# A fused attention layer in Strassen quads: normalised inputs laid out token by token, and four output products carried over in PSUM

## The chip, the core and the metric

The kernel runs on one core of a Trainium2 chip. A core has five engines with queues of their own: TensorE (matrix products, written PE in the profile, its weight loads PEld), VectorE (DVE), ScalarE (ACT), GpSimd (POOL) and SyncE (SP). They share SBUF, the working memory of 128 partitions, and PSUM, eight banks that TensorE writes its products to. DMA engines move data between SBUF and DRAM. The metric is device time in microseconds (us), lower is better.

## The reference

Eight sequences of 256 tokens with 512 features, all in float32. Cut to what matters:

```python
x = hidden_states                                  # (8, 256, 512)
xn = (x - mean(x)) / sqrt(var(x) + 1e-5)           # over the 512 features
q, k, v = xn @ wq.T, xn @ wk.T, xn @ wv.T          # 32, 8 and 8 heads of 128
q, k = rope(q), rope(k)
scores = q @ k.T / sqrt(128) * scale + causal      # one k head for 4 q heads
s = softmax(scores) @ v                            # (8, 256, 4096)
s = s @ wo.T                                       # back to 512 features
# experts: 4 of rank 16, each token takes the best two
gates = softmax(top2(xn @ router_w.T))
delta = sum_e gates_e * 4.0 * (xn @ A_e.T) @ B_e.T
out = x + s * silu(delta)
```

## The kernel before

The sequences are handled in four blocks of two (`tb`, 0 to 3). Within a block the heads go in eight groups (`g`, 0 to 7; one key head and four query heads).

**Products in quads.** Projections and the output projection use a scheme of seven products instead of eight for a 2 x 2 split (Strassen in Winograd's form). A quad of 512 output features for two sequences is cut into 2 x 2 by features of the input (`half`) and by sequence (`b`); the sums of weights (S1 to S4) are formed once, kept in DRAM and loaded again by the later blocks. The input's sums are formed by `add_up` into `XT`. In `quad` (lines 575 to 656) products 1, 2 and 3 read the normalised input `XB` itself and products 4 to 7 a sum in `XT`. Names in the trace: `pa`, `pe` and `pd` are the three PSUM banks of a quad, followed by q, k or v. One product is four matmuls of 128 x 128 x 256 that the profile shows as eight records, since a float32 matmul runs in two passes. For queries and keys the input is the moving operand, which streams through the array; for values (`rows`) it is the stationary one, loaded as weights.

**How the normalised input comes.** `norm` (lines 318 to 478) loads `x`, takes mean and variance and normalises, tokens on partitions. The products need the features on partitions. In the first block TensorE transposes and ScalarE copies from PSUM (`turn`, `read`). In the later three VectorE transposes 32 x 32 blocks (`turn_blocks`), `spread` writes them to DRAM (`turned`, four DMAs a sequence) and `gather` loads them to `XB` (four DMAs a sequence). These DMAs are issued by SyncE, in one queue with the stores and loads that turn the softmax's result (`there<-blocks`, `pT<-there`). `XB` has one buffer: `gather` for the next block waits until the last product of this block that reads `XB` is done.

**Attention.** `softmax` computes scores (`sc`), exponentials and sums, transposes 32 x 32 blocks and sends them through DRAM to `pT`; `values` multiplies with `v` (`av`, copied to `a`).

**Output projection.** `out_project` (lines 944 to 1020) forms for each group seven products `po` in PSUM, each of which is added to an accumulator `acc` 1 to 7 in SBUF (`add_up`: ScalarE copies in the first group, VectorE adds after that). At the end of a block `put_together` combines the seven accumulators into the four quarters of the output, multiplies with the gates `g` (loaded from DRAM) and adds the input `xf`. For the last group of the last block `last_products` (lines 1022 to 1161) does this by hand: the accumulators of the first seven groups are put together (`put`) while TensorE still works, and the last group's products stay in PSUM: 1, 6, 7 and 4 follow each other in one bank `oa`, copied aside by ScalarE in between; 2 stands in `oe`, 5 in `od`, and 3 comes in two halves (`o3_0`, `o3_1`). `result` adds a sum of these to the accumulator, multiplies by the gate and adds the input, three VectorE operations.

**What sets the order.** `Plan` (lines 170 to 257) is a planner that runs when the program is built. TensorE's pieces are laid in an order written out by hand (lines 1413 to 1459); every other job gets a due time from the pieces that need it, an estimated duration and a lag, and is put into its engine's queue when a small simulation finds it ready. The estimates fix only the order. `hold` and `Room` keep account of buffers, `ps_mm` with four banks among them (tag `mm`). Engines work through their queues strictly in this order.

`experts` computes the router and the experts; `route` reads `XB` as the stationary operand (`lme`).

Nearly all instructions are recorded by one helper, so the profile gives line 118 for them; tiles and operations tell them apart.

Of the kernel before, what the change touches and what calls it, by code (L numbers as in the profile page):

```python
# [260 lines left out]
def layer(ctx: ExitStack, tc: tile.TileContext, x, wquad, woquad, raT, bT, table, out):  # L261
# [53 lines left out]

    def norm(tb):

# [47 lines left out]
        def new_acts():  # L367
            acts[tb] = (
                one.tile([P, NB, 2, 2, S], F32, tag="XB", name=f"XB{tb}"),
                one.tile([P, 4, 2, S], F32, tag="XT", name=f"XT{tb}"),  # L370
            )

        def read(b, half):
            if b == half == 0:
                new_acts()
            nc.scalar.copy(acts[tb][0][:, b, half], box["p", b, half])

        def turn_blocks(t):
# [3 lines left out]
                to.rearrange("p (q k t s) -> p t k q s", q=NQ, k=DC, t=2)[:, t % 2],  # L382
# [14 lines left out]
        def gather(b):  # L397
            if b == 0:
                new_acts()
            to = acts[tb][0][:, b].rearrange("p h c (t a s) -> p a (h c t) s", t=2, a=NQ)  # L400
            for a in range(NQ):
                nc.sync.dma_start(
                    out=to[:, a],
                    in_=box["there", b][:, :, a, :].rearrange("q r (k s) -> (q r) k s", s=BLK),
                )

        def add_up(i):
            XB, XT = acts[tb]
            b11, b12, b21, b22 = (XB[:, b, h] for h in range(2) for b in range(NB))
# [35 lines left out]
        if tb:  # L445
            for b in range(NB):
# [6 lines left out]
                    add("sp", 2.4, lambda b=b: gather(b), after=[out_] + reads[:1],  # L453
# [121 lines left out]
    def quad(tb, which, out, room, rows, name):  # L575
# [15 lines left out]
        def product(bank, i, half, b, t, first):  # L591
# [3 lines left out]
            xb = acts[tb][0][:, b, half] if t is None else acts[tb][1][:, t]  # L595
# [172 lines left out]
    free_p = [None]  # L768
# [175 lines left out]
    def out_project(tb, g):  # L944
# [19 lines left out]
        for i, (to, a, b, op) in enumerate(Features.steps):  # L964
# [4 lines left out]
            )  # L969
        if (tb, g) == (NTB - 1, KV - 1):  # L970
# [3 lines left out]
        def product(k, a, w):  # L974
            box = {}

            def work():
                ps = box["ps"] = ps_mm.tile([P, 2, 2 * P], F32, tag="mm", name=f"po{n}_{k}")
                for t in range(2):
                    for h in range(2):  # L980
                        nc.tensor.matmul(
                            ps[:, t, :], lhsT=abox[a]["a"][:, h, bass.ts(t, P)],
                            rhs=wbox[w][:, h, :], start=t == h == 0, stop=h == 1,
# [12 lines left out]

            h = hold("mm")
            p = add("pe", 1.73, work, after=[a_done[a], w_done[w]], opens=[h], closes=[ah[a], wh[w]])
            if g == 0:
# [20 lines left out]
        return [pieces[k] for k in (1, 2, 6, 5, 7, 4, 3)]  # L1020

    def last_products(n, abox, ah, a_done, wbox, wh, w_done):

# [4 lines left out]
        turn = []  # L1028

        def put(to, a, b):  # L1030
            turn[:] = [
                dve(lambda: nc.vector.tensor_add(M[to]["s"], M[a]["s"], M[b]["s"]),
                    turn + [M[k]["done"] for k in (to, a, b)])
            ]
            M[to]["done"] = turn[0]
# [455 lines left out]
```

## Time and profile before

| | |
|---|---|
| time, median of three runs | 1338.13 us (1336.35 to 1342.35) |
| profiled execution | 1336.8 us, its span 1334.9 us |
| instructions | 20259 |
| matmuls of queries, keys and values that read `XB` | 1152 records of 128 x 256 |
| matmuls that read `XT` | 1536 records |
| DMA traffic | 282.14 MB, 211 GB/s |
| DMA packets | 143402, of them under 512 bytes 41856 |
| loads `XB<-turned` | 24 of 128 KB, median 4.9 us from issue to landing |
| loads `pT<-there` | 128 of 384 KB, median 5.5 us |

The span is the time from the first to the last instruction that the profile shows; the rest of the execution's time lies around it. "Records" are the entries of the profile: a float32 matmul has two. A busy time counts overlapping records of an engine once. A record's duration is its latency; the next one starts before it ends, so the pace of a stream is read from how long a run of records takes together. The granted clock of TensorE was 0.999 of full speed over the execution.

### The profile page before, as it was taken

The page shows a single profiled execution, that of the slowest core. Times are in us where ns is not written, and L with a number is a line of the kernel's source. Part 1 is how long each engine was busy: PE and PEld are TensorE (multiplying, and loading weights), DVE is VectorE, ACT ScalarE, POOL GpSimd, SP SyncE. Part 2 cuts the span into 40 slices and gives each one's busy share as a digit, 9 for nine tenths or more (in the row PEclk, how much of TensorE's full clock was granted, in tenths as well). Part 3 has the DMA queues.
Part 4 walks back from the last instruction along what each step waited for, and adds up shares of the span by engine and source line. Part 5 has one row for each costly group of instructions (what it writes and reads, how often), then busy time and mean ns, then how long its engine had stood idle before and what let it go on. Part 6 is the DMA issues. An engine that isn't in the chain of part 4 may idle for free.

```text
span 1334.9 us, 20259 instructions
## 1 busy us (share of the span) xinstructions
PE 1323.2 (99%) x6488; PEld 1166.7 (87%) x6488; DVE 1046.9 (78%) x2515; ACT 700.5 (52%) x1896; POOL 314.6 (24%) x579
## 2 busy tenths in 40 slices
PE   8999999999999999999999999999999999999998
PEld 7888888888889888888888988888888888888886
DVE  6798888986978658688597875968858787685987
ACT  3485455554645546465454564546544455544751
POOL 2332222222221122221222212222122221222010
PEclk9999999999999999999999999999999999999999
DMA  6497666696766765768766666576866676566583
GB/s 213 159 294 245 208 219 217 203 266 217 229 191 207 214 212 177 228 205 246 220 192 221 209 209 206 174 249 201 235 222 192 211 221 208 180 194 198 161 293 109
DMA packets 143402, 282.14 MB, mean 211 GB/s; under 512 B 41856, under 2 KB 81920, under 8 KB 143296
## 3 DMA queue, kind: packets, MB, share of 16 engines
q0 software_dynamic: 45760, 149.98, 36.5%
q1 hardware_dynamic: 97312, 130.20, 31.4%
q8 instruction: 53, 0.87, 0.3%
q10 hardware_dynamic: 224, 0.66, 0.2%
q14 instruction: 53, 0.43, 0.1%
HBM read 197.94 MB, written 82.84 MB: 210 GB/s over the span
## 4 chain that ended last, share of the span: by engine, by line
PE 97%; DVE 1%; DMA 1%; SPq 1%; issue 0%; DVEq 0%; ACT 0%
PE po L118 28%; PE paq L118 17%; PE av L118 12%; PE sc L118 10%; PE pdq L118 8%; PE peq L118 4%; PE pav L118 4%; PE pak L118 4%; PE pdk L118 2%; PE pdv L118 2%; PE dle L118 1%; PE pev L118 1%; PE lme L118 1%; PE pek L118 1%; SPq L118 1%; DMA pT<-there 1%
## 5 line engine op out<-in xcount | busy, mean ns | idle before, releaser
L118 ACT ACTIVATE p<-z,least 128x256 f32<-128x256 f32 (+7 forms) x512 | 207.2, 406 | 138.0 <-DVE least L118 107.1
L118 PE MATMUL po<-wo,a 128*128 128x256 f32 x992 | 233.5, 379 | 0.0
L118 PEld LDWEIGHTS po<-wo,a 128*128 128x128 f32 x992 | 186.6, 190 | 22.9
L118 PE MATMUL av<-pT,v 128*128 128x256 f32 x768 | 186.4, 380 | 1.5 <-DMA pT<-there 1.4
L118 DVE CUSTOM_DVE_ANT_0 z<-sc,tab 128x256 f32<-128x256 f32 (+7 forms) x512 | 132.9, 301 | 67.1 <-PE sc L118 63.9
L118 PE MATMUL paq<-XT,w 128*128 128x256 f32 x768 | 181.7, 379 | 0.0
L118 PE MATMUL po<-wo,s 128*128 128x256 f32 x744 | 177.5, 382 | 0.0
L118 PEld LDWEIGHTS sc<-kk,qTq 128*128 128x128 f32 x1024 | 159.0, 191 | 12.8 <-DVE p L118 0.8
L118 DVE TENSOR_TENSOR acc<-acc,po 128x512 f32<-128x512 f32 x189 | 127.8, 677 | 52.7 <-PE po L118 51.8
L118 PE MATMUL sc<-kk,qTq 128*128 128x256 f32 (+7 forms) x1024 | 167.7, 302 | 0.0
L118 PEld LDWEIGHTS av<-pT,v 128*128 128x128 f32 x768 | 145.3, 190 | 22.1 <-issue 2.7
L118 PEld LDWEIGHTS paq<-XT,w 128*128 128x128 f32 x768 | 145.0, 190 | 18.9 <-ACT p1q L118 0.2
L118 ACT COPY a<-av 128x512 f32<-128x512 f32 x128 | 74.6, 583 | 163.3 <-PE av L118 162.8
L118 PEld LDWEIGHTS po<-wo,s 128*128 128x128 f32 x744 | 139.4, 190 | 22.6 <-issue 5.3
L118 POOL DMA_DIRECT2D w<-sums x144 | 79.0, 549 | 334.9 <-PE paq L118 129.7
L118 POOL DMA_DIRECT2D w<-in_wquad_dram x148 | 81.0, 548 | 259.7 <-PE paq L118 84.8
L118 ACT COPY swq<-cq 64x1024 f32<-64x1024 f32 x128 | 133.6, 1044 | 4.6 <-DVE kk L118 2.3
L118 DVE STREAM_TRANSPOSE blocks<-p 128x1024 f32<-128x1024 f32 (+1 forms) x128 | 122.8, 965 | 3.9 <-DMA there<-blocks 2.0
L118 ACT ACTIVATE p<-p,total 128x160 f32<-128x160 f32 (+4 forms) x320 | 91.9, 363 | 27.2 <-DVE total L118 26.5
L118 DVE TENSOR_TENSOR qTq<-cq,tab 128x1024 f32<-128x1024 f32 x64 | 77.7, 1213 | 29.8 <-ACT cq L118 29.6
L118 ACT ACTIVATION_READ_ACCUMULATOR p<-z,least 128x1 f32 x512 | 95.9, 187 | 0.0
L118 POOL DMA_DIRECT2D wo<-in_woquad_dram x104 | 57.2, 551 | 130.3 <-PE po L118 125.1
(138 smaller groups left out, 1905.7 us busy)
## 6 DMA issues: line engine op xcount, KB each, us to landing
there<-blocks SPq DMA_DIRECT2D x256, 192.0 KB, 4.2
pT<-there SPq DMA_DIRECT2D x128, 384.0 KB, 5.5
w<-in_wquad_dram POOLq DMA_DIRECT2D x148, 256.0 KB, 4.5
w<-sums POOLq DMA_DIRECT2D x144, 256.0 KB, 4.2
wo<-in_woquad_dram POOLq DMA_DIRECT2D x104, 256.0 KB, 5.0
wo<-osums POOLq DMA_DIRECT2D x96, 256.0 KB, 4.6
sums<-w POOLq DMA_DIRECT2D x48, 256.0 KB, 4.6
osums<-wo POOLq DMA_DIRECT2D x32, 256.0 KB, 4.4
```

Of the source, the lines that this page charges most:

```text
L118: ins = what(*args, **kwargs)
```

## The change

Two parts. The first changes the layout of `XB` from (sequence, half, chunk, token) to (sequence, token, chunk), with chunk the innermost of four feature chunks; `half_of` gives the same view as before, two chunks by 256 tokens, in which a step from token to token is now four float32 values. The writers follow: ScalarE's copy in the first block, the output side of `turn_blocks`, and `gather`, which issues two DMAs for a sequence in pieces of 128 values in place of four in pieces of 32. The planner's estimate for them goes from 2.4 to 1.0.

The second keeps four products of group 6 of the last block out of the accumulators. Products 1, 2 and 5 stay in their PSUM banks, and the last group's 1, 2 and 5 are added on top of them; product 4 of group 6 is not formed in its own place but in front of product 4 of the last group, into the same bank. The accumulators 1, 2, 4 and 5 so end one group earlier; `put` loses its chain of turns, four accumulators are multiplied by the gate and given the input beforehand (`prepare`; before it was one), and `result` is two operations in place of three. The order of the last group's pieces is 1, 5, 6, 2, 7, half of 3, both 4, half of 3 in place of 1, 2, 6, 5, 7, half of 3, 4, half of 3.

```diff
@@ -313,10 +313,13 @@
         nc.scalar.dma_start(out=tab, in_=table)
         nc.scalar.dma_start(out=bt, in_=bT)
 
+    def half_of(tb, b, h):
+
+        return acts[tb][0][:, b, :, 2 * h : 2 * h + 2].rearrange("p t c -> p c t")
+
 
 
...
@@ -366,20 +369,20 @@
 
         def new_acts():
             acts[tb] = (
-                one.tile([P, NB, 2, 2, S], F32, tag="XB", name=f"XB{tb}"),
+                one.tile([P, NB, S, DC], F32, tag="XB", name=f"XB{tb}"),
                 one.tile([P, 4, 2, S], F32, tag="XT", name=f"XT{tb}"),
             )
 
         def read(b, half):
             if b == half == 0:
                 new_acts()
-            nc.scalar.copy(acts[tb][0][:, b, half], box["p", b, half])
+            nc.scalar.copy(half_of(tb, b, half), box["p", b, half])
 
         def turn_blocks(t):
 
             to = xs["x", t // 2].rearrange("p t d -> p (t d)")
             nc.vector.transpose(
-                to.rearrange("p (q k t s) -> p t k q s", q=NQ, k=DC, t=2)[:, t % 2],
+                to.rearrange("p (q t s k) -> p t k q s", q=NQ, k=DC, t=2)[:, t % 2],
                 box[t].rearrange("p (k q s) -> p k q s", q=NQ, s=BLK),
             )
 
@@ -397,16 +400,16 @@
         def gather(b):
             if b == 0:
                 new_acts()
-            to = acts[tb][0][:, b].rearrange("p h c (t a s) -> p a (h c t) s", t=2, a=NQ)
-            for a in range(NQ):
+            to = acts[tb][0][:, b].rearrange("p (t a s) k -> p t a (s k)", t=2, a=NQ)
+            for t in range(2):
                 nc.sync.dma_start(
-                    out=to[:, a],
-                    in_=box["there", b][:, :, a, :].rearrange("q r (k s) -> (q r) k s", s=BLK),
+                    out=to[:, t],
+                    in_=box["there", b].rearrange("q r a (t e) -> t (q r) a e", t=2)[t],
                 )
 
         def add_up(i):
-            XB, XT = acts[tb]
-            b11, b12, b21, b22 = (XB[:, b, h] for h in range(2) for b in range(NB))
+            XT = acts[tb][1]
+            b11, b12, b21, b22 = (half_of(tb, b, h) for h in range(2) for b in range(NB))
             t1, t2, t3, t4 = (XT[:, k] for k in range(4))
 
             a, b = ((b12, b11), (b22, t1), (b22, b12), (b21, t2))[i]
@@ -450,7 +453,7 @@
                 ]
                 out_ = add("sp", 2.4, lambda b=b: spread(b), after=turns, closes=[xh[b]], lag=3.4)
                 reads += [
-                    add("sp", 2.4, lambda b=b: gather(b), after=[out_] + reads[:1],
+                    add("sp", 1.0, lambda b=b: gather(b), after=[out_] + reads[:1],
                         opens=[] if b else [x_hold[tb]], lag=7.0)
                 ] * 2
         for b, half in [] if tb else ((0, 0), (0, 1), (1, 0), (1, 1)):
@@ -592,7 +595,7 @@
             if first:
                 box[bank] = new(bank)
             ps = box[bank]
-            xb = acts[tb][0][:, b, half] if t is None else acts[tb][1][:, t]
+            xb = half_of(tb, b, half) if t is None else acts[tb][1][:, t]
 
             for m in range(2):
                 for c in range(2):
@@ -765,7 +768,7 @@
 
 
 
-    free_p = [None]
+    fused = {}
 
     def softmax(tb, g, b):
 
@@ -967,6 +970,7 @@
                 after=[a_done[a], a_done[b]] + Features.before(i, a_done),
                 opens=[ah[to]] if to != S3 else [], closes=[ah[a], ah[b]],
             )
+        fuse = (tb, g) == (NTB - 1, KV - 2)
         if (tb, g) == (NTB - 1, KV - 1):
             return last_products(n, abox, ah, a_done, wbox, wh, w_done)
         pieces = {}
@@ -974,13 +978,15 @@
         def product(k, a, w):
             box = {}
 
-            def work():
-                ps = box["ps"] = ps_mm.tile([P, 2, 2 * P], F32, tag="mm", name=f"po{n}_{k}")
+            def work(first=True):
+                if first:
+                    box["ps"] = ps_mm.tile([P, 2, 2 * P], F32, tag="mm", name=f"po{n}_{k}")
+                ps = box["ps"] if first else box["ps"]()
                 for t in range(2):
                     for h in range(2):
                         nc.tensor.matmul(
                             ps[:, t, :], lhsT=abox[a]["a"][:, h, bass.ts(t, P)],
-                            rhs=wbox[w][:, h, :], start=t == h == 0, stop=h == 1,
+                            rhs=wbox[w][:, h, :], start=first and t == h == 0, stop=h == 1,
                             skip_group_check=True,
                         )
 
@@ -994,8 +1000,24 @@
                     s = acc[tb, k]["s"]
                     nc.vector.tensor_add(s, s, box["ps"])
 
+            if fuse and k == 4:
+
+                def onto(bank, after):
+                    box["ps"] = bank
+                    return add(
+                        "pe", 1.73, lambda: work(False), after=[a_done[a], w_done[w]] + after,
+                        closes=[ah[a], wh[w]],
+                    )
+
+                fused[k] = onto
+                return
             h = hold("mm")
             p = add("pe", 1.73, work, after=[a_done[a], w_done[w]], opens=[h], closes=[ah[a], wh[w]])
+            if fuse and k in (1, 2, 5):
+
+                fused[k] = box, h, p
+                pieces[k] = p
+                return
             if g == 0:
                 acc[tb, k] = {"hold": hold("acc"), "done": None}
             mine = acc[tb, k]
@@ -1017,25 +1039,32 @@
                 sums_of["wo", g, i].near = (pieces[1], 0.0)
         if g == KV - 1:
             put_together(tb)
-        return [pieces[k] for k in (1, 2, 6, 5, 7, 4, 3)]
+        return [pieces[k] for k in ((1, 2, 6, 7, 5, 3) if fuse else (1, 2, 6, 5, 7, 4, 3))]
 
     def last_products(n, abox, ah, a_done, wbox, wh, w_done):
+
 
 
         tb = NTB - 1
         M = {k: acc[tb, k] for k in range(1, 8)}
         dve = lambda what, after, **kw: add("dve", 0.61, what, after=after, **kw)
-        turn = []
-
-        def put(to, a, b):
-            turn[:] = [
-                dve(lambda: nc.vector.tensor_add(M[to]["s"], M[a]["s"], M[b]["s"]),
-                    turn + [M[k]["done"] for k in (to, a, b)])
-            ]
-            M[to]["done"] = turn[0]
-
-        for to, a, b in ((2, 1, 2), (6, 1, 6), (7, 6, 7), (3, 3, 5), (3, 3, 6), (4, 7, 4), (5, 7, 5)):
-            put(to, a, b)
+        puts = []
+
+        def put(to, a, b, after=()):
+            M[to]["done"] = dve(
+                lambda: nc.vector.tensor_add(M[to]["s"], M[a]["s"], M[b]["s"]),
+                [M[k]["done"] for k in (to, a, b)] + list(after),
+            )
+            puts.append(M[to]["done"])
+
+        put(2, 1, 2)
+        put(3, 3, 5)
+        read5 = puts[-1:]
+        put(6, 1, 6)
+        put(3, 3, 6)
+        put(7, 6, 7)
+        put(5, 7, 5, read5)
+        put(4, 7, 4)
         box, loads = {}, {}
 
         def load(what, b):
@@ -1061,19 +1090,28 @@
 
         def prepare(k, b, f):
             s = lambda: M[k]["s"]
-            m = dve(lambda: gate(s(), s(), b, f), [M[k]["done"], turn[0], loads["g", b]])
+            m = dve(lambda: gate(s(), s(), b, f), [M[k]["done"], loads["g", b]])
             M[k]["done"] = dve(
                 lambda: nc.vector.tensor_add(s(), s(), box["xf", b][:, :, bass.ts(f, 2 * P)]),
                 [m, loads["xf", b]],
             )
 
-        prepare(4, 1, 0)
+        for k, b, f in ((2, 0, 0), (3, 0, 1), (5, 1, 1), (4, 1, 0)):
+            prepare(k, b, f)
 
         banks = {}
 
         def product(bank, a, w, first, after, opens=(), ts=(0, 1)):
+            before = fused.get(bank)
+            along = before and bank not in banks
+            if along:
+                banks[bank] = None
+                after = after + [before[2]]
+
             def work():
-                if first:
+                if along:
+                    banks[bank] = before[0]["ps"]
+                elif first:
                     banks[bank] = ps_mm.tile([P, 2, 2 * P], F32, tag="mm", name=f"{bank}{n}")
                 for t in ts:
                     for h in range(2):
@@ -1110,34 +1148,33 @@
 
         def result(k, b, f, what, first):
 
-            s = lambda: M[k]["s"]
-            r = dve(
-                lambda: nc.vector.tensor_add(s(), s(), box[what]), turn + [first, M[k]["done"]]
-            )
-            m = dve(lambda: gate(s(), s(), b, f), [r, loads["g", b]])
+            m = dve(lambda: gate(box[what], box[what], b, f), [first, loads["g", b]])
             return dve(
-                lambda: nc.vector.tensor_add(s(), s(), box["xf", b][:, :, bass.ts(f, 2 * P)]),
-                [m, loads["xf", b]],
-            )
-
-        oa, oe, od, o3, o4 = (hold("mm") for _ in range(5))
-        p1 = product("oa", A11, A11, True, [], [oa])
+                lambda: nc.vector.tensor_add(M[k]["s"], M[k]["s"], box[what]), [m, M[k]["done"]]
+            )
+
+        oa, oe, od = (fused[k][1] for k in (1, 2, 5))
+        for k, bank in ((1, "oa"), (2, "oe"), (5, "od")):
+            fused[bank] = fused[k]
+        o3, o4 = (hold("mm") for _ in range(2))
+        p1 = product("oa", A11, A11, False, [])
         c1 = aside("p1", p1)
-        p2 = product("oe", A12, A21, True, [], [oe])
+        p6 = product("oa", S2, S2, False, [c1])
+        c6 = aside("u2", p6)
+        p2 = product("oe", A12, A21, False, [p6])
         e = bank_and("p1", "oe", [p2, c1], [oe])
         store(lambda: M[2]["s"], 0, 0, p2, [result(2, 0, 0, "p1", e)])
-        p6 = product("oa", S2, S2, False, [c1])
-        c6 = aside("u2", p6)
-        p5 = product("od", S1, S1, True, [], [od])
+        p5 = product("od", S1, S1, False, [])
         d = bank_and("u2", "od", [p5, c6], [od])
         pre = result(3, 0, 1, "u2", d)
         p7 = product("oa", S3, A12, False, [c6])
         c7 = aside("u3", p7)
         d = bank_and("u3", "od", [p5, c7], [od])
         store(lambda: M[5]["s"], 1, 1, p7, [result(5, 1, 1, "u3", d)])
-        p4 = product("oa", A22, S4, False, [c7])
+        before4 = fused[4](lambda: banks["oa"], [c7])
+        p4 = product("oa", A22, S4, False, [before4])
         m = dve(
-            lambda: gate(M[7]["s"], banks["oa"], 1, 0), [p4, M[7]["done"], turn[0], loads["g", 1]],
+            lambda: gate(M[7]["s"], banks["oa"], 1, 0), [p4, M[7]["done"], loads["g", 1]] + puts,
             closes=[oa],
         )
         r = dve(lambda: nc.vector.tensor_add(M[4]["s"], M[4]["s"], M[7]["s"]), [m, M[4]["done"]])
@@ -1148,7 +1185,7 @@
             p = product(bank, S4, A22, True, [after], [h], (t,))
             m = dve(
                 lambda: gate(M[6]["s"][:, t, :], banks[bank][:, t, :], 0, 1, t),
-                [p, M[6]["done"], turn[0], loads["g", 0]], closes=[h],
+                [p, M[6]["done"], loads["g", 0]] + puts, closes=[h],
             )
             r = dve(
                 lambda: nc.vector.tensor_add(M[3]["s"][:, t, :], M[3]["s"][:, t, :], M[6]["s"][:, t, :]),
@@ -1158,7 +1195,7 @@
             return p
 
 
-        return [p1, p2, p6, p5, p7, half(0, o3, p7), p4, half(1, o4, p4)]
+        return [p1, p5, p6, p2, p7, half(0, o3, p7), before4, p4, half(1, o4, p4)]
 
     def put_together(tb):
         M = {k: acc[tb, k] for k in range(1, 8)}
@@ -1238,13 +1275,12 @@
         box = {}
 
         def route(t):
-            XB = acts[tb][0]
             if not box:
                 box["lm"] = ps_av.tile([P, NT, E + E * R], F32, tag="av", name=f"lm{n}")
             for c in range(DC):
                 nc.tensor.matmul(
                     box["lm"][:, t, :],
-                    lhsT=XB[:, t // 2, c // 2, c % 2, bass.ts(t % 2, P)],
+                    lhsT=half_of(tb, t // 2, c // 2)[:, c % 2, bass.ts(t % 2, P)],
                     rhs=ra[:, c, :],
                     start=(c == 0),
                     stop=(c == DC - 1),
```

More of the change, by code (lines that the diff above doesn't have):

```diff
@@ L1111, in result @@
         def result(k, b, f, what, first):
-            s = lambda: M[k]["s"]
-            r = dve(
-                lambda: nc.vector.tensor_add(s(), s(), box[what]), turn + [first, M[k]["done"]]
-            )
-            m = dve(lambda: gate(s(), s(), b, f), [r, loads["g", b]])
-            return dve(
-                lambda: nc.vector.tensor_add(s(), s(), box["xf", b][:, :, bass.ts(f, 2 * P)]),
-                [m, loads["xf", b]],
-            )
-        oa, oe, od, o3, o4 = (hold("mm") for _ in range(5))
-        p1 = product("oa", A11, A11, True, [], [oa])
+            m = dve(lambda: gate(box[what], box[what], b, f), [first, loads["g", b]])
+            return dve(
+                lambda: nc.vector.tensor_add(M[k]["s"], M[k]["s"], box[what]), [m, M[k]["done"]]
+            )
+        oa, oe, od = (fused[k][1] for k in (1, 2, 5))
[3 more added lines that the diff above has]
+        p1 = product("oa", A11, A11, False, [])
         c1 = aside("p1", p1)
-        p2 = product("oe", A12, A21, True, [], [oe])
+        p6 = product("oa", S2, S2, False, [c1])
+        c6 = aside("u2", p6)
+        p2 = product("oe", A12, A21, False, [p6])
         e = bank_and("p1", "oe", [p2, c1], [oe])
         store(lambda: M[2]["s"], 0, 0, p2, [result(2, 0, 0, "p1", e)])
-        p6 = product("oa", S2, S2, False, [c1])
-        c6 = aside("u2", p6)
-        p5 = product("od", S1, S1, True, [], [od])
+        p5 = product("od", S1, S1, False, [])
         d = bank_and("u2", "od", [p5, c6], [od])
```

## The prediction

> **What bounds the kernel now.** I read the page's busy times first, then the waits of TensorE, then TensorE by stage, then the chain of waits and the timelines around the two places that the change touches.
>
> ```profile
> PE 1323.2 (99%) x6488; PEld 1166.7 (87%) x6488; DVE 1046.9 (78%) x2515; ACT 700.5 (52%) x1896; POOL 314.6 (24%) x579
> ...
> PE av L118 <- DMA pT<-there: 1.4, 1, 1.4
> PE warm L118 <- POOL ident masks.py:199: 1.4, 1, 1.4
> PE xp L118 <- DVE xn L118: 1.3, 2, 1.0
> PE pdk L118 <- DVE XT L118: 1.0, 1, 1.0
> PE pak L118 <- ACT XB L118: 0.2, 1, 0.2
> ```
>
> TensorE is busy for 1323.2 of 1334.9 us. The 11.7 us that are left are the start-up (most of it before 18 us), one wait of 1.4 us for a load of `pT`, and the stretch behind the last matmul. The last is in the table by stage (its first row's PE figure is the busy time, the clock stands behind POOL):
>
> ```profile
> 1316.00:1328.60 12.60, 12.57 (x58) 10.56 (x56) 11.86 (x20) 1.76 (x3) 0.00 (x0) 1.00 0.13 44
> 1328.60:1335.00 6.40, 0.00 (x0) 0.00 (x0) 2.97 (x7) 0.00 (x0) 0.00 (x0) 0.81 0.37 123
> ```
>
> TensorE ends at 1328.6; then VectorE works 2.97 us more, and the last store lands at 1334.9. So work taken from VectorE or the queues is worth at most a few us, while each ns added to a matmul of the many is paid in full. How long one takes is read from pieces of the chain, eight records of 256 columns in 1.73 us, or 216 ns each, and sixteen of 68 columns in 1.74 us, 109 ns each:
>
> ```profile
> 37.65 1.73 PE paq L118 x8
> 409.10 1.74 PE lme L118 x16
> ```
>
> **The one stall, and what the two loads do to it (gain 1.4 us).** SyncE's queue, where the `pT` load waited:
>
> ```profile
> 281.67 6.83 SPq L118 DMA_DIRECT2D XB<-turned  x4
> 289.25 2.20 SPq L118 DMA_DIRECT2D there<-blocks  x4
> 291.49 4.67 SPq L118 DMA_DIRECT2D XB<-turned  x4
> 296.26 3.11 SPq L118 DMA_DIRECT2D pT<-there  x2
> ...
> 296.26 7.60 DMA pT<-there
> ```
>
> The eight loads of `XB` hold the queue for 6.83 + 4.67 = 11.5 us; each scatters 1024 pieces of 128 bytes (128 partitions, 8 pieces). The `pT` load behind the second four goes out at 296.26 and takes 7.60 us against a median of 5.5 for its kind, and the `av` matmul waits for it until 304.00. The changed program issues two loads per sequence, 512 pieces of 512 bytes each: 4096 pieces become 1024. If the time on the queue goes by pieces, 4.67 becomes 1.2; if by issues, 2.3. Its order on the queue also changes: both sequences' loads now stand ahead of the `there` stores, so nothing of `XB` lies between those stores and `pT`. The stores ended at 291.45 and land after a median of 4.2 us, at about 295.7: the load can start 0.6 us sooner, and at the median 5.5 instead of 7.60 lands 2.1 us sooner still, 2.7 together against a wait of 1.41. I take the whole 1.4; the lower bound is 0. In the next two blocks of sequences the same loads take 4.49 + 3.82 and 4.32 + 3.68 us and TensorE shows no wait there, so nothing more is won. The products that read `XB` begin at 292.1 while the loads go out near 282 and land in some 5 us, so moving the second sequence's load forward costs nothing visible.
>
> **The end (gain 1.8 us).** The timeline of the last matmul and of VectorE behind it:
>
> ```profile
> 1327.54 1.03 PE L118 MATMUL o<-wo,s 128*128 128x256 f32 x4
> 1327.75 0.41 DVE L118 SCALAR_TENSOR_TENSOR acc<-o,g 128x256 f32<-128x256 f32 x1
> 1328.08 0.68 DVE L118 SCALAR_TENSOR_TENSOR acc<-acc,g 128x512 f32<-128x512 f32 x1
> ...
> 1329.62 0.68 DVE L118 SCALAR_TENSOR_TENSOR acc<-oa,g 128x512 f32<-128x512 f32 x1
> 1330.22 0.41 DVE L118 SCALAR_TENSOR_TENSOR acc<-o,g 128x256 f32<-128x256 f32 x1
> 1330.55 1.01 DVE L118 TENSOR_TENSOR acc<-acc,acc 128x512 f32<-128x512 f32 x2
> ```
>
> The first half's matmul `o` ended at 1325.90 and VectorE came to it at 1327.75: it is 1.85 us behind. The last half's end, 1328.57, is answered at 1330.22. One 512-column operation follows the last every 0.60 us, a 256-column one every 0.33. The change takes four add-ups from VectorE (products 1, 2, 5 and 4 of the last but one group) and one of three operations from each of three results, and adds six (the gate and the input on accumulators 2, 3 and 5): 4 + 3 - 6, one less, or 0.6 us. What counts is that those six now stand ahead of the last products. TensorE has the same matmuls, so I keep its end at 1328.57 and lay the new order backwards from it: half, 4 of the last group, 4 of the one before, half, 7, 2, 6, 5, 1, each product 1.73. Product 3 of the last but one group then ends near 1314.6. VectorE has nine operations left on the accumulators from there, 5.4 us, to 1320.0, then the three results, which it reaches soon after their products end (7 ends at 1323.2, its copy at 1323.8). By 1327.1 it has nothing left but the two last. Product 4 ends at 1327.70: gate to 1328.35, add to 1328.95, then the last half, 0.33 + 0.42, to 1329.7. Before it was 1331.56: 1.86 us, say 1.8. Bounds: nothing, if VectorE is late all the same (its cover between 1320 and 1327 is only about 0.6 us), and 2.2, if it waits for nothing but 1328.57 + 0.75. The copy between product 7 and the next into the same bank is covered by one half, 0.865 us, as before, and TensorE waited 0.21 there. Three banks stay open from the last but one group on, so its products 6, 7, 5 and 3 share one or two; between the products that follow each other in a bank stand 1.3 us of `av` and another product of 1.73, against an add-up of 0.68. I cost it at nothing; without that cover it is about 0.7 us for each of two products. SyncE's stores stay five, the last two as close together as before.
>
> **The layout (0 taken, up to 220 us).** A token's four feature chunks now lie side by side, so what reads one chunk of `XB` steps over four values, 16 bytes, from column to column; before, columns were adjacent. These read it: the moving side of products 1, 2 and 3 of each query and key quad (`paq`, `peq`, `pdq` 256 records each, `pak`, `pek`, `pdk` 64 each: 960), the weight side of the value quads (192 loads) and of `lme` (128 loads), and sixteen VectorE sums into `XT`. ScalarE's four start-up copies and twelve VectorE transposes write so.
>
> ```profile
> L118 PE MATMUL paq<-XB,w x256: 379/379/463, 26.6 to 1248.1; 128*128 128x256 f32 x128
> L118 PE MATMUL paq<-XT,w x768: 379/379/463, 30.1 to 1262.4; 128*128 128x256 f32 x192
> ```
>
> Both rows have adjacent columns, from either tile the same 379 ns; no row of TensorE in this trace steps, so the price lies between two ends. Lower end: nothing, 216 ns as now. Upper end: each column takes two steps instead of one, 432 ns; the nearest row with so slow a column is `lme`, 109 / 68 = 1.6 ns, or 410 ns for 256. At 432 it is 960 x 216 = 207 us. Weight loads of 128 values at twice 109 ns cost `lme` 128 x 109 = 14 us, and the value quads almost nothing (218 beside a matmul of 216). All of it is on the path, since TensorE never waits. I take the lower end, because the row nearest in everything but the step is `paq<-XB` itself: a column takes 0.84 ns there, and no row shows whether a second step would fit into that. It is the choice that I am least sure of. The sums and copies, at 0.68 and 0.59 us, cost the start-up up to 0.6 each for one copy and one sum on its path, 1.2; later ones are off it. Taken at 0.
>
> The Trainium skill (SBUF — State Buffer, Door 1: The DMA port swizzle, the remark on cachelines) speaks against the change: lines are 16 bytes, and a stream needs at least two hits in a line for its full rate, which a step of four fp32 never gives; yet the same remark calls four fp32 a step that is free. Its table for VectorE (Vector Engine (DVE) Microarchitecture Reference, 5.2 Measured stream behaviour on trn2) has 1.73 ns a column instead of 1.05 for single hops; an estimate from that page for TensorE is 443 ns a record, and the sum would be about +218 us for the moving side. The trace has no such read and decides nothing.
>
> **Sum.** 1336.8 (the profiled execution, 1.3 under the median of 1338.13) - 1.4 - 1.8 = 1333.6; at the median 1338.1 - 3.2 = 1335. Own range 1332 to 1339: both gains nothing plus the start-up's 1.2 above, and below the gains plus the 1.8 by which runs lie under the median. I call 0.5%, 6.7 us, what can be told from no change.
>
> **Rivals.** (a) The step is paid in full by TensorE: 1335 + 207 + 14 = 1556, slower. For it: 99% busy, no cover. Against it: two passes per matmul already give a column 0.84 ns. (b) It is paid in part: each 10 ns on a record is 9.6 us, so from 10 ns (5%) on the kernel is slower beyond doubt; 1345 to 1500. The same place, but a buffer that hides most. (c) The loads don't do what they should: time on the queue goes by issues, other loads crowd the DMA engines (0.6 to 0.8 busy on the page), and the 1.4 us come back at another wait: 1338.1 - 1.8 = 1336.3. (d) The new order of the queue also saves waits that the modelled matmul ends hide: under 1331.4; only 11.7 us are idle in all.
>
> **How the numbers follow.** Forecast 0.40, (a) 0.32, (b) 0.16, (c) 0.08, (d) 0.04. The likeliest is 1335. Within 0.5%: 0.40 + 0.08 = 0.48; slower 0.32 + 0.16 = 0.48; faster 0.04. The range has to reach (a): 1331 to 1560.
>
> **What would show it.** Records of `paq<-XB` at 379 ns and eight in 1.73 us: forecast; a longer row for `XB` beside an unchanged one for `XT`: (a) or (b), by its size. Two loads of `XB` in 1 to 2.5 us on SyncE's queue and no wait of `av` for `pT` near 304: the first gain; that wait at another place: (c). The last VectorE operation within 1.2 us of TensorE's end: the second. It is wrong if TensorE's busy time leaves 1323 us by more than 7.

## The result, and the profile after

| | before | after |
|---|---|---|
| time, median | 1338.13 us (1336.35 to 1342.35) | 1577.64 us (1576.52 to 1578.89, 4 runs) |
| span of the profiled execution | 1334.9 us | 1574.7 us |
| TensorE busy | 1323.2 us | 1567.8 us |
| TensorE idle within the span | 11.7 us | 6.9 us |

The ratio of the times is 1.1785, with an interval of 1.1756 to 1.1814: the changed kernel is 18% slower. The forecast was 1335 us, and even the range's upper end, 1560, lies below the result.

The page of the changed kernel, its line of busy times and the granted clock in 40 slices (tenths of full speed, 9 is 90% or more), then the waits of TensorE (what waited, for what, us in total, times, longest):

```profile
PE 1567.8 (100%) x6488; PEld 1210.2 (77%) x6488; DVE 1065.3 (68%) x2514; ACT 706.2 (45%) x1896; POOL 314.0 (20%) x579
...
PEclk9999999999999999999999999999999999999999
```

```profile
PE warm L118 <- POOL ident masks.py:199: 1.4, 1, 1.4
PE pak L118 <- ACT XB L118: 0.7, 1, 0.7
PE xp L118 <- DVE xn L118: 0.7, 1, 0.7
```

The waits got shorter, the clock is as good as full (0.998), the number of TensorE's instructions is the same, and it is busy for 244.6 us more. So the same instructions must take longer. Which ones is in the trace by tile, `XB` first and `XT` second (minimum, median and maximum of one in ns, then first and last start in us):

```profile
L118 PE MATMUL paq<-XB,w x256: 612/632/678, 34.8 to 1486.0; 128*128 128x256 f32 x128
L118 PEld LDWEIGHTS lme<-ra,XB x128: 307/329/332, 17.0 to 1278.4; 128*128 128x128 f32 x128
```

```profile
L118 PE MATMUL paq<-XT,w x768: 377/379/462, 42.1 to 1502.5; 128*128 128x256 f32 x192
L118 DVE TENSOR_TENSOR XT<-XB x8: 1043/1088/1127, 18.0 to 1147.2; 128x512 f32<-128x512 f32 x8
```

`XT` kept its layout and its 379 ns. A record that streams `XB` rose to 632 ns; it was 379 as well. Those are latencies; the pace is in the chain (start, us together, what, number of records):

```profile
17.24 3.68 PE lme L118 x16
...
51.59 3.62 PE pdq L118 x8
55.21 1.83 PE pev L118 x8
57.05 1.73 PE pav L118 x8
```

Eight moving records of `XB` take 3.62 us, 452 ns each in place of 216; `lme`, whose weights step, takes 230 in place of 109; a value product of `XB` takes 1.83 in place of 1.73, because there the stepped side is the weight load, which runs beside a matmul of 216 ns. The sum: 960 x (452.5 - 216) = 227 us, 128 x (230 - 109) = 15.5, 192 x 12 = 2.3 (a record of 229 in place of 217), together 245 us. TensorE's busy time rose by 244.6. Its idle time fell by 4.8 (2.2 at the end, 1.4 the wait for `pT`, the rest in the start-up), and 244.6 - 4.8 is the 239.8 us by which the span grew. The sum closes to within what these readings can tell, about 1 us.

Around the two places of the intended gains. SyncE's queue in the changed kernel (start, us on the queue):

```profile
341.81 3.71 SPq L118 DMA_DIRECT2D XB<-turned  x4
...
349.85 1.86 SPq L118 DMA_DIRECT2D there<-blocks  x4
...
355.09 1.34 SPq L118 DMA_DIRECT2D pT<-there  x2
```

Both sequences' loads hold the queue for 3.7 us in place of 11.5, stand ahead of the stores, and nothing of `XB` stands between the stores and `pT`; no wait for `pT` is left. The end of the timeline:

```profile
1569.51 1.03 PE L118 MATMUL o<-wo,s 128*128 128x256 f32 x4
...
1571.04 0.42 DVE L118 SCALAR_TENSOR_TENSOR acc<-o,g 128x256 f32<-128x256 f32 x1
1571.49 0.42 DVE L118 TENSOR_TENSOR acc<-acc,acc 128x256 f32<-128x256 f32 x1
```

VectorE finishes at 1571.91, 1.4 us behind TensorE's last matmul (1570.54), where it was 3.0 before.

### The profile page after: what moved, and what is told of

Same layout as the page of the kernel before. It is cut to its first block, busy times and chain, and to the rows that moved or that the text cites. A ratio compares the mean times of both kernels' runs of the same rounds, so it can differ in the third digit from the quotient of the medians.

```text
span 1574.7 us, 20234 instructions
## 1 busy us (share of the span) xinstructions
PE 1567.8 (100%) x6488; PEld 1210.2 (77%) x6488; DVE 1065.3 (68%) x2514; ACT 706.2 (45%) x1896; POOL 314.0 (20%) x579
## 4 chain that ended last, share of the span: by engine, by line
PE 99%; DVE 0%; DMA 0%; ACT 0%; issue 0%
PE po L118 25%; PE paq L118 18%; PE pdq L118 11%; PE av L118 11%; PE sc L118 9%; PE peq L118 7%; PE pak L118 5%; PE pav L118 4%; PE pdk L118 3%; PE pek L118 2%; PE pdv L118 2%; PE lme L118 2%; PE dle L118 1%; PE pev L118 1%; DMA x<-in_x_dram 0%; DVE acc L118 0%
## 5 line engine op out<-in xcount | busy, mean ns | idle before, releaser
L118 PE MATMUL po<-wo,a 128*128 128x256 f32 x1024 | 241.1, 379 | 0.0
L118 PEld LDWEIGHTS po<-wo,a 128*128 128x128 f32 x1024 | 192.9, 190 | 26.2 <-issue 2.4
L118 PE MATMUL po<-wo,s 128*128 128x256 f32 x760 | 181.1, 382 | 0.0
L118 PEld LDWEIGHTS po<-wo,s 128*128 128x128 f32 x760 | 143.5, 191 | 33.9 <-issue 17.5
L118 PE MATMUL paq<-XB,w 128*128 128x256 f32 x256 | 122.5, 635 | 0.0
L118 PE MATMUL pdq<-XB,w 128*128 128x256 f32 x256 | 121.8, 632 | 0.0
L118 PE MATMUL peq<-XB,w 128*128 128x256 f32 x256 | 121.6, 631 | 0.0
```

Of the source, the lines that this page charges most:

```text
L118: ins = what(*args, **kwargs)
```

## The experiments

Seven experiments are versions of the whole kernel, timed against the kernel before on the same chip; two more, at the end, are small kernels that only measure.

| kernel | median us | ratio to before, interval |
|---|---|---|
| `e1_tail_only` | 1335.01 | 0.9983, 0.9973 to 0.9993 |
| `e2_tail_order` | 1342.90 | 1.0040, 1.0028 to 1.0053 |
| `e8_unpacked` | 1333.93 | 0.9976, 0.9968 to 0.9985 |
| `e4_tensor_packed` | 1334.91 | 0.9980, 0.9971 to 0.9989 |
| `e3_layout_only` | 1580.65 | 1.1810, 1.1783 to 1.1838 |
| `e5_weights_stepped` | 1355.65 | 1.0127, 1.0103 to 1.0151 |
| `e6_step_of_two` | 1343.84 | 1.0041, 1.0029 to 1.0052 |

The first four shared runs of the kernel before with a median of 1337.86, the last three, on another chip, with one of 1338.13. Diffs are against the changed kernel.

### One part at a time: `e1_tail_only` and `e3_layout_only`

The new end with the old layout, and the new layout with the old end:

```diff
 # e1_tail_only
     def half_of(tb, b, h):
-        return acts[tb][0][:, b, :, 2 * h : 2 * h + 2].rearrange("p t c -> p c t")
+        return acts[tb][0][:, b, h]
...
-                one.tile([P, NB, S, DC], F32, tag="XB", name=f"XB{tb}"),
+                one.tile([P, NB, 2, 2, S], F32, tag="XB", name=f"XB{tb}"),
...
-            for t in range(2):
+            for a in range(NQ):
```

```diff
 # e3_layout_only
-        fuse = (tb, g) == (NTB - 1, KV - 2)
...
-        return [p1, p5, p6, p2, p7, half(0, o3, p7), before4, p4, half(1, o4, p4)]
+        return [p1, p2, p6, p5, p7, half(0, o3, p7), p4, half(1, o4, p4)]
```

> The old layout of XB with its four loads a sequence, and the changed end (four products kept in PSUM, results in two operations). Theory: the end alone is worth what the trace of the changed kernel shows behind TensorE's last matmul, 4.2 us in place of 6.3, so about 1336 us, and the wait of 1.4 us of av for pT in the second block stays. Rival: the layout and not the new order shortened the end (fewer transfers beside it), then this one stands at 1338 us, no faster than before.

> The layout of the change with its two loads a sequence, and the end as before. Theory: the two parts add up: 1577.6 + 2 = 1580 us. Rival: the parts act on each other (the slower quads leave VectorE time, so the end has nothing to save): 1577.6 us, the same as the changed kernel.

The end alone takes 1335.01 us, 2.9 less than before (by the interval 0.9 to 3.6). The layout alone takes 1580.65, 3.0 more than both together; but the intervals of the two ratios overlap (1.1783 to 1.1838, 1.1756 to 1.1814), and its granted clock was lower (0.994 to 0.996, in the changed kernel 0.997 to 0.998). The traces tell more: from TensorE's last matmul to the end of the span it is 6.4 us in the kernel before and 6.1 in `e3_layout_only`, 4.3 in `e1_tail_only` and 4.1 in the changed kernel. So the end is worth 2 us or a little more in either company, and the whole loss is in the layout. The wait for `pT` is still there in `e1_tail_only`, in three pieces (us in total, times, longest), together even a little longer:

```profile
PE av L118 <- DMA pT<-there: 2.0, 3, 1.3
```

### TensorE's reads or the rest of the layout: `e4_tensor_packed` and `e5_weights_stepped`

Loads, copies, transposes and sums as in the changed kernel, but TensorE reads the same bytes as if they lay in the old order, without a step (so it multiplies other values, the same number of them); in the second one only the weight sides keep the step.

```diff
+    def packed_of(tb, b, h):
+        flat = acts[tb][0][:, b].rearrange("p t c -> p (t c)")
+        return flat[:, 2 * h * S : 2 * (h + 1) * S].rearrange("p (c t) -> p c t", c=2)
...
 # e4_tensor_packed
-            xb = half_of(tb, b, half) if t is None else acts[tb][1][:, t]
+            xb = packed_of(tb, b, half) if t is None else acts[tb][1][:, t]
...
-                    lhsT=half_of(tb, t // 2, c // 2)[:, c % 2, bass.ts(t % 2, P)],
+                    lhsT=packed_of(tb, t // 2, c // 2)[:, c % 2, bass.ts(t % 2, P)],
...
 # e5_weights_stepped
-            xb = half_of(tb, b, half) if t is None else acts[tb][1][:, t]
+            xb = (half_of if rows else packed_of)(tb, b, half) if t is None else acts[tb][1][:, t]
```

> The changed kernel with one thing different: the matmuls of TensorE read 512 adjacent values of XB for each half where they should pick two of four chunks (other values, the same number), for the moving and the stationary side; transfers, transposes, copies and VectorE's sums keep the step. Theory: the whole loss is the step in TensorE's reads: 960 moving records back from 452 to 216 ns (227 us), 128 loads of lme back from 230 to 109 ns (15 us), value quads 2 us: 1577.6 - 244 = 1334 us, up to 1337. Rival: part of the loss comes with the layout elsewhere (VectorE's and ScalarE's stepped operands, late inputs); then it stays above 1345 us.

> The changed kernel, but the moving side of the query and key quads reads adjacent values (other values, the same number); only the weight loads of the value quads and of lme step. Theory: weight loads take twice as long too, but only where nothing hides them: lme 128 x 121 ns = 15.5 us, value quads 192 x 12 ns = 2.4 us, so 1334 + 18 = 1352 us. Rival: weight loads slow the matmuls before them through the same port; then the value quads lose much more here than the 2.4 us, and the time lies above 1360 us.

Without the step TensorE's busy time is back where it was, and the time, 1334.91, is that of the new end alone. The page's busy times and TensorE's waits in `e4_tensor_packed`:

```profile
PE 1322.7 (99%) x6488; PEld 1166.8 (88%) x6488; DVE 1056.0 (79%) x2514; ACT 702.3 (53%) x1896; POOL 315.8 (24%) x579
```

```profile
PE pak L118 <- ACT XB L118: 1.6, 1, 1.6
...
PE av L118 <- DMA pT<-there: 0.2, 1, 0.2
```

VectorE's sums and transposes and ScalarE's copies are as slow here as in the changed kernel, and the time can't be told from that of `e1_tail_only` (1335.01): the fewer loads save 1.8 us of the wait for `pT`, and about half of it is lost again, in the start-up, in part because the first product waits for a whole sequence in this version, and at the end (4.7 us behind the last matmul in place of 4.3).

The step in the weights alone costs 20.7 us more than `e4_tensor_packed`, where 15.5 + 2.3 = 18 were worked out. TensorE's idle time is no part of the difference: it is 9.5 us in `e5_weights_stepped` and 9.3 in the other; a longer wait for `pT` (1.6 and 0.2) is made up in the start-up. Its busy time is 20.6 us longer, and for 1.7 of that the trace has a cause of another kind: from 416.78 to 420.19 us the granted clock was 0.50, and eight records of `pdq` without a step took 3.43 us there in place of 1.73. What is left, about 1 us, the readings can't tell apart.

### The order of the queue without fewer pieces: `e2_tail_order` and `e8_unpacked`

The first is `e1_tail_only` with the planner's estimate for `gather` at 1.0, so that both sequences' loads go ahead of the stores, still as eight loads of 128-byte pieces. The second takes the two loads of 512-byte pieces into the buffer of `XT`, and lets ScalarE copy them into the old `XB`:

```diff
 # e2_tail_order, against e1_tail_only
-                    add("sp", 2.4, lambda b=b: gather(b), after=[out_] + reads[:1],
+                    add("sp", 1.0, lambda b=b: gather(b), after=[out_] + reads[:1],
...
 # e8_unpacked
+        def unpack(b, half):
+            nc.scalar.copy(
+                acts[tb][0][:, b, half],
+                staged(b).rearrange("p (t k) -> p k t", k=DC)[:, 2 * half : 2 * half + 2],
+            )
```

> As the kernel with the changed end alone, but the planner's estimate for the loads of XB is 1.0 as in the change, so that both sequences' loads stand ahead of the stores of there on SyncE's queue; still four loads a sequence in pieces of 128 bytes. Theory: the stall of 1.4 us came from the place on the queue, so it is gone here, 1334.7 us. Rival: it came from the many small pieces, then it stays or moves to another wait, 1336 us or more.

> The two loads a sequence go token by token into XT's buffer, which is free at that time, and ScalarE copies them into the old layout of XB (four copies in each of three blocks, reading with a step of 16 bytes); TensorE and VectorE read adjacent columns; the changed end is kept. Theory: TensorE sees no step, so all that the change could bring is here: about 1334.5 us, since twelve copies of about 1.1 us lie on an engine that is busy 52% of the time. Rival: the copies make the first products of a block late, then TensorE shows waits there and the time is 1336 to 1342 us.

`e2_tail_order` is slower than before. The wait for `pT` is gone, as the theory had it, but the rival holds: the wait moved to another place, and the time is far above 1336. Three readings of it, SyncE's queue, VectorE's timeline (in brackets the idle time before, and what ended it) and the waits of TensorE:

```profile
281.69 11.62 SPq L118 DMA_DIRECT2D XB<-turned  x8
293.41 2.59 SPq L118 DMA_DIRECT2D there<-blocks  x4
```

```profile
301.23 1.25 DVE L118 STREAM_TRANSPOSE blocks<-p 128x1024 f32<-128x1024 f32 x1 [2.91 <-DMA there<-blocks]
302.39 0.65 DVE L118 TENSOR_TENSOR XT<-XB 128x512 f32<-128x512 f32 x1
```

```profile
PE pdk L118 <- issue: 7.5, 3, 3.1
```

Eight loads hold the queue for 11.62 us, so the stores behind them go out at 293.41 (in the kernel before at 289.25). VectorE's next transpose needs the buffer that they empty, and behind it in VectorE's queue stands the sum `XT<-XB` that TensorE's next product reads. TensorE stands still before it, in each of the three later blocks (2.2, 3.1 and 2.2 us), and after the first two halts it works for 3.4 us at a granted clock of 0.50. Together the idle and the busy time account for the whole difference: 5.0 us more of the one and 4.5 of the other than in `e1_tail_only`, whose span is 9.5 us shorter. The first halt and what follows it (the clock is the third figure from the end of the table by stage, whose columns are the stretch, its length, and the busy us of TensorE, its weight loads, VectorE, ScalarE and GpSimd):

```profile
302.00:303.10 1.10, 0.00 (x0) 0.00 (x0) 1.10 (x3) 0.00 (x0) 0.00 (x0) 1.00 0.86 252
303.10:304.00 0.90, 0.85 (x2) 0.80 (x3) 0.90 (x2) 0.00 (x0) 0.00 (x0) 0.50 0.42 164
304.00:305.00 1.00, 1.00 (x4) 0.73 (x4) 1.00 (x6) 0.38 (x1) 0.00 (x0) 0.50 0.46 107
```

There eight records of `pdk`, without any step, took 3.62 us from 303.15 on: the same number as in the changed kernel from another cause, which only the clock tells apart. That standing still brings the lower clock on is not shown: it didn't after the third halt, and in `e5_weights_stepped` the clock fell while TensorE was busy. The kernels with the two short loads have the new order without such a halt (the changed kernel, `e4_tensor_packed`, `e8_unpacked`), so the new order hurts only where the loads are long.

`e8_unpacked` beats both kernels, 1333.93 us. Its interval overlaps that of `e1_tail_only`, so no gain over the end alone is shown. Its trace is of the slowest of its eleven runs, 1338.44 us, and has a wait for `pT` of 2.1 us with 3.4 us at half the granted clock behind it; what the faster runs look like was not seen.

### Where the price of a step begins: `e6_step_of_two`, `e7_steps`, `e9_lines`

In `e6_step_of_two` the two chunks of one half lie side by side, a step of two values; four loads of 256-byte pieces a sequence:

```diff
-        return acts[tb][0][:, b, :, 2 * h : 2 * h + 2].rearrange("p t c -> p c t")
+        return acts[tb][0][:, b, h].rearrange("p t c -> p c t")
...
-                one.tile([P, NB, S, DC], F32, tag="XB", name=f"XB{tb}"),
+                one.tile([P, NB, 2, S, 2], F32, tag="XB", name=f"XB{tb}"),
```

The two small kernels stream 32 records of 256 columns (or 32 weight loads of 128 columns) for each way of stepping, one after the other. Their core:

```python
def stepped(k, n):
    return src[:, : n * k].rearrange("p (n k) -> p k n", k=k)[:, 0]
def rows(first, hop, run, n):
    return src[:, : n // run * hop].rearrange("p (n k) -> p n k", k=hop)[:, :, first : first + run]
...
for k, name in names.items():
    read(columns(name, stepped(k, N)))
...
read(columns("inside", rows(1, 8, 2, N)))
read(columns("across", rows(3, 8, 2, N)))
```

`stepped` takes every k-th value (`e7_steps`), `rows` runs of adjacent ones (`e9_lines`): pairs at words 1 and 2 of every eight, and at 3 and 4.

> The changed kernel with the two chunks of a half side by side in place of all four: columns step by 8 bytes, and each aligned 16 bytes are used for two columns in a row; four loads a sequence in pieces of 256 bytes. Theory of the line: what costs is that each column opens another 16 bytes; with two columns in each the matmuls run at 216 ns, and the time is 1334 to 1337 us. Rival, any step costs: the price goes with the distance, so half of it at 8 bytes, about 1455 us; or any step costs all, 1577 us. The page SBUF - State Buffer of the Trainium skill (Door 1: The DMA port swizzle) asks for two hits in a line, which speaks for the first.

> Nothing of the layer is computed: one tile of inputs is read by sixteen matmuls (32 records) of 256 columns with steps of 1, 2, 3, 4, 5, 6, 8 and 16 values, by pairs of adjacent values with a hop of 16 or 64 bytes (aligned to 8 bytes, and once not), by weight loads with the same steps, and by copies of VectorE and ScalarE that step on the read or on the write side. Theory of the line: steps of 1 and 2 and aligned pairs run at 216 ns a record, steps of 4 and more at 452 ns, and 3 between them. Rival, distance: the price grows from 4 to 16 values. Rival, any step: 2 values already cost 452 ns. For the copies on VectorE and ScalarE: 512 values with a step of 4 took 1.07 to 1.12 us in the changed kernel against 0.59 to 0.69, so about 2 ns a value from step 4 on.

> Nothing of the layer is computed: 32 records of 256 columns for each pattern, read from one tile. The steps measured before fit one rule, a column costs the larger of 0.84 ns (216 ns for 256) and 1.76 ns for each new 16 bytes that it opens. Theory of the 16-byte line: pairs of adjacent values with a hop of 32 bytes run at 227 ns where both lie in one line (first value 0 of 4) and also at first value 1 of 4, and at 451 ns where they lie across two lines (first value 3); runs of four with a hop of 32 bytes at 217 ns inside a line and 227 ns across two; two streams taken in turn, 8 KB apart, at 216 ns if the port keeps two lines open and 451 ns if it keeps one, four streams likewise. Rival, a grain of 8 bytes: first value 1 would have cost as much as first value 3. For bfloat16 (one record a matmul, 0.42 ns a column) the same price per line: 32 records at 107 to 113 ns for steps of 1 and 2 values, 226 ns for 4, 338 ns for 6 and 451 ns from 8 on; rival, a price per value that steps: 107 ns up to some step, then twice that.

The step of two isn't free, and `e6_step_of_two` missed by 7 us what was expected. Its groups by line and form (busy us, mean ns of one, idle before), and two pieces of its chain:

```profile
L118 PE MATMUL paq<-XT,w 128*128 128x256 f32 x768 | 181.7, 379 | 0.0
L118 PE MATMUL paq<-XB,w 128*128 128x256 f32 x256 | 64.8, 394 | 0.0
```

```profile
27.18 1.81 PE paq L118 x8
30.80 1.73 PE paq L118 x8
```

1.81 us for eight is 226 ns, 10 more than 216; over 960 records that is 10 us, and it takes the end's gain and more. TensorE's busy time is 11.6 us longer than in `e1_tail_only`. The chain of `e7_steps` has the whole curve (32 records each; the name is the step in values):

```profile
13.39 6.91 PE mov_one L44 x32
20.30 7.25 PE mov_two L44 x32
27.55 10.88 PE mov_three L44 x32
38.44 14.44 PE mov_four L44 x32
...
81.88 14.72 PE mov_eight L44 x32
96.60 13.80 PE mov_sixteen L44 x32
...
131.84 3.52 PE wei_one L50 x32
...
145.29 7.45 PE wei_four L50 x32
```

A record takes 216, 227, 340, 451, 460 and 431 ns at steps of 1, 2, 3, 4, 8 and 16: it rises up to a step of four and then no more. A weight load takes 110 ns at step 1 and 233 at step 4. The granted clock was 1.00 for all the moving records and for `wei_one`, but 0.50 for `wei_four`; that 233 is the price of the step and not of the clock rests on `lme` in the changed kernel, 230 ns at the full clock. The chain of `e9_lines` tells what is counted:

```profile
12.97 7.36 PE mov_inside L50 x32
20.33 14.43 PE mov_across L50 x32
...
42.12 6.91 PE mov_four_inside L50 x32
49.03 7.25 PE mov_four_across L50 x32
56.28 8.74 PE mov_two_streams L50 x32
65.03 14.07 PE mov_four_streams L50 x32
79.10 3.50 PE mov_half_one L50 x32
...
86.22 7.25 PE mov_half_four L50 x32
...
104.36 14.46 PE mov_half_eight L50 x32
```

Pairs at words 1 and 2 cost 230 ns a record, pairs at words 3 and 4, which lie in two stretches of 16 bytes, 451. In bfloat16 it takes a step of eight values, again 16 bytes, to reach 452 (at a granted clock of 0.50; the last section comes back to it). The prices by lines stood in the expectation and hold, except for the streams by turns (last section). To within 5% one rule gives the float32 figures of both chains: a float32 record takes the longer of 0.84 ns for each column and 1.76 ns for each new 16-byte line that its columns open. Step 2 opens a line for every second column, 0.88 ns a column; step 3 for three columns of four, 1.32; step 4 for each, 1.76, and 256 x 1.76 = 451 ns. The rival grain of 8 bytes would have made the pair at words 1 and 2 as dear as the pair at words 3 and 4.

## Why the prediction was wrong

**The layout: the step that failed.** "I take the lower end, because the row nearest in everything but the step is `paq<-XB` itself." No other row could carry that choice, and that row could not either: the step was the only thing that changed. TensorE had no idle time to hide it in. In place of nothing, the step cost 236 ns a record, 227 us over the 960, and TensorE's busy time left 1323 us by 244.6, where the prediction took 7 for the sign of being wrong. The mechanism is that of rival (a), the step paid in full by every record that reads `XB`: `e4_tensor_packed` takes the step alone away, and with it 243 us.

**Its upper end was short too.** 432 ns assumed that each column takes two steps in place of one. In its place stands a price per line, 452 ns in the kernel: 960 x 20 = 19 us more. `lme` was priced at 218 ns and took 230 (1.5 us), and the value quads 2.3 us where "almost nothing" stood. The three add 23 us to the rival's 1556 and make it 1579, beside the 1577.64 measured. That `lme`, taken for a row with a slow column of 1.6 ns, came so near is luck: its pace is that of its weight loads. In `e7_steps` 64 columns with a weight load each go at the same 110 ns as its 68, and in the changed kernel it went to 230 ns when only the weights stepped.

A rule of the Trainium skill had weighed against the change there (SBUF — State Buffer, Door 1: The DMA port swizzle: 16-byte lines, at least two hits in a line for the full rate), and the runs agree with its size of line: 227 ns at two hits, near the full 216, and 451 at one. Its remark that four fp32 are a step without cost is contradicted by the same 451 ns; the measurement decides.

**The stall: right as far as it can be seen.** The changed kernel has no wait for `pT`, two loads hold the queue for 1.86 us (between the 1.2 by pieces and the 2.3 by issues), and the order is as laid out. But TensorE's slower pace there gives every load more time; with the old pace the wait was 0.2 us in `e4_tensor_packed` and 1.6 in `e5_weights_stepped`. So the 1.4 us aren't a firm gain, and that the changed kernel shows no wait at all may be slack that its loss bought. That moving the second sequence's load forward "costs nothing visible" holds for short loads only; `e2_tail_order` shows the price with long ones.

**The end: right in kind, and in size by some luck.** 1.8 us were worked out, with 2.2 as the bound; the stretch behind the last matmul went from 6.4 to 4.1 us, and the runs give 2.9 (0.9 to 3.6). The sum for it is VectorE's alone, and there it was a little high: VectorE follows TensorE by 1.4 us where 1.1 had been laid out, so 1.6 us of the gain are its, and the sign of 1.2 us was missed. The other 0.6 us, from VectorE's end to the span's, were in no sum (3.4 before, 2.7 now); with the same end it is 2.9 in `e1_tail_only` and 3.3 in `e4_tensor_packed`, so they are no firm gain. No wait of the products in shared banks appears.

**The start-up: right.** Sums went from 0.68 to 1.09 us and ScalarE's copies from 0.59 to 1.11, as the bound of 1.2 allowed for one of each; the waits in it fell by about 1 us all the same. The 1.0 us of `pdk` for `XT` is gone, since the stepped products ahead of it take longer; the wait of `pak` for ScalarE rose from 0.2 to 0.7; that of `xp` lies between 0.2 and 1.3 us from trace to trace, and its change says nothing. In the range, 1332 comes from 1333.6, which already lay 1.3 under the median; from 1335 the same 1.8 us lead to 1333.

## What to carry to other kernels

Lay SBUF out for whoever reads it most often, not for the DMA that writes it: 24 loads were made cheaper here, and 1280 reads on the bound engine paid. When an edit changes the access pattern of an instruction and no row of the profile has that pattern, the old row is no evidence for the price; with that engine at 99% the choice between the ends is the whole forecast, and a kernel of 32 records would settle it. When such a layout is wanted for its loads, let an engine with time to spare turn it back: `e8_unpacked` does that at no loss, though no gain over the end alone is shown. And when loads are moved forward in a queue, count how long they hold it.

## What the runs showed of the hardware

- A stream without step slows when the granted clock falls (`e2_tail_order`: eight records in 3.62 us at 0.50, 1.73 at full); one that opens a line for each column doesn't. In the changed kernel the clock was 0.50 from 493.9 to 497.3 and from 883.0 to 886.4 us, and eight stepped records there took 3.66 and 3.71 us, beside 3.62 to 3.69 for most others:

```profile
493.40 3.66 PE pdq L118 x8
...
883.48 3.71 PE pdq L118 x8
```

The weight loads at a step of four agree (230 ns at full in `lme`, 233 at 0.50 in `e7_steps`), while those at a step of three went from 173 to 213 ns from start to start when the clock fell in their midst. In `e9_lines` the bfloat16 records at a step of eight, from 104.36 us on, ran at half the clock throughout (table by stage), so their price at the full clock was not measured:

```profile
104.00:118.00 14.00, 14.00 (x33) 3.87 (x31) 0.00 (x0) 0.16 (x1) 0.00 (x0) 0.50 0.00 0
```

- A float32 matmul shows as two records of 216 ns for 256 columns, a bfloat16 one as a single record of 109 (`mov_half_one` in `e9_lines`), a quarter of the time in all.
- One line is not all that is kept. Columns taken by turns from two places far apart cost 273 ns a record, where one open line would give 451 and two 216; from four places 440. Why 273 stays open.
- ScalarE and VectorE pay for steps too, in proportion less; that it goes by lines was not tested there. In `e7_steps` a ScalarE copy of 256 columns takes 402 ns at a step of one, 418 at two, 530 at three and 651 at four when it reads, and 401 to 668 when it writes; on VectorE 288 to 372 and 286 to 394. For VectorE the Trainium skill (Vector Engine (DVE) Microarchitecture Reference, 5.2 Measured stream behaviour on trn2) asks for adjacent pairs from an 8-byte boundary on, and gives a pair at an odd word a price of its own; on TensorE a pair at an odd word was 230 ns inside a line and 451 across two. No run here tried that on VectorE.
